# Attention of a two-layer block: values divided after 32 by 32 transposes on VectorE, rows of the mixture turned on TensorE, masks on ScalarE

## Chip, core and metric

The kernel runs on one core of a Trainium2 chip. The metric is the device time of one execution in microseconds (us). Engines: PE is TensorE, DVE is VectorE, ACT is ScalarE, POOL is GpSimd, SP is the engine whose queue issues most DMAs.

## What is computed

A block of two layers over x (8, 256, 256): an auto-correlation attention, a feed-forward layer with balanced experts, a multi-head attention over the context, and a mixture of 8 experts with the best two per token and a shared part. The change lies in the third, and in what hands its rows to the fourth:

```python
def _L1_xattn_ref(x, data, Wq, bq, Wkv, bkv, Wp, bp):
    # 8 batches, 256 queries, 256 keys, 16 heads of d = 16
    q = (x @ Wq + bq).reshape(bs, n_ctx, HEADS, d)
    kv = (data @ Wkv + bkv).reshape(bs, n_data, HEADS, 2 * d)
    k, v = (kv[..., :d], kv[..., d:])
    scores = jnp.einsum('bqhd,bkhd->bhqk', q, k) * scale
    attn = jax.nn.softmax(scores, axis=-1)
    out = jnp.einsum('bhqk,bkhd->bqhd', attn, v).reshape(bs, n_ctx, WIDTH)
    return out @ Wp + bp
...
    x = x + _L1_xattn_ref(_layernorm(x, axis=-1), ctx_1024, ...)
    x = x + _L1_ffn_ref(_layernorm(x, axis=-1), ...)
```

All numbers are float32. A general path for unusual inputs is in the program too and isn't executed here.

## The kernel before

Tokens lie on partitions: X holds 16 tiles of 128 tokens, batch b has tiles 2b and 2b + 1 (TPB = 2). The 16 heads are in NB = 2 columns c of 8; within a column head 2g + m has the 32 partitions of group g, and m picks one of two halves. Every instruction is issued in the order of the source on its engine's queue; the helpers below are called from one loop over b and c (L3018), written out by hand so that each engine finds work of another batch while it waits.

For batch b, in (b, 0) and (b, 1):
- scores (L2666): per block of 128 keys, four products of 32 rows each into two tiles of the pool ps_s, then two Exp on ScalarE into ex.
- values (L2685), one step later: 16 products of the keys' values with ex into pv. VA has 16 values, a column of ones and zeros per head, so that pv holds in each group of 32 partitions the 16 sums and, in the 17th row, the divisor.
- keep (L2698): DVE copies pv to ov. turn_back (L2702): TensorE turns ov of a batch in 8 transposes, DVE takes reciprocals and multiplies into on. turn_out (L2725): TensorE turns on back in 4 transposes, DVE copies to oT. project_out (L2737): 8 products with wp, DVE adds to X.
- turn_q (L2628) and queries (L2632) prepare the next batch: 4 transposes of the normalised rows, a copy hT, 4 products, and for each c two masked copies QM (m = 0 by ScalarE, m = 1 by DVE; for b + 1 = 1 both by DVE).
- batch_stats and norm_m write the normalised rows of batch b - 2, HP, for the mixture: statistics on DVE, powers and norms on POOL. take_apart_m (L2770) lets ScalarE part their 16-bit halves, two DMA transposes on SP's queue turn them, and join_m (L2785), one batch later, lets ScalarE join them to HT. The last two batches are turned by TensorE (turn_m, L2757, with the helper turn_pair, L2615) after the loop.
- route (L2843), a generator whose steps are called from b = 4 on (`gates`): per four tiles, TensorE's logits pl, a turn pt, DVE's choice of two experts (some 25 small instructions), counts pc on TensorE. send (L2939) then scatters one tile's rows to Td with an indirect DMA of POOL's queue, one after another.

PSUM has eight banks: ps_m has three tiles of one bank for turns, queries, projection and route; ps_s two tiles of two banks; ps_v one tile for pv.

After the loop the shared experts' first products (classic_up, L3237, tiles from ps_s) alternate with turn_back, turn_out and project_out of batch 7, turn_m and the last routes; then the experts run, whose rows are loaded from Td (load_rows, L3543).

Of the kernel before, what the change touches and what calls it, by code (L numbers as in the profile page):

```python
# [1086 lines left out]
def fast_path(  # L1087
# [1376 lines left out]
    for e in range(E - 1):  # L2464
        if e == 5:

            wpv = L1_xattn_Wp.rearrange("(c g m d) n -> m g d c n", c=NB, g=4, m=2)
            for m in range(2):
                for g in range(4):
                    r0 = 64 * m + DH * g  # L2470
                    nc.sync.dma_start(out=wp[r0 : r0 + DH], in_=wpv[m, g])
                    nc.sync.dma_start(
                        out=bvc[r0 : r0 + DH, :],
                        in_=bkv[:, 1, :].rearrange("(c g m) d -> m g d c", c=NB, g=4)[m, g],
                    )
# [67 lines left out]
    ps_m = banks.enter_context(tc.tile_pool(name="ps_m", bufs=3, space=PSUM))  # L2543
    ps_s = banks.enter_context(tc.tile_pool(name="ps_s", bufs=2, space=PSUM))
    ps_v = banks.enter_context(tc.tile_pool(name="ps_v", bufs=1, space=PSUM))
# [86 lines left out]
    def queries(b, c, eng=nc.scalar):  # L2632
        if c == 0:
            QM[b] = pq2.tile([P, NB, 2, S], F32, tag="QM", name="QM")
        pp = ps_m.tile([P, S], F32, tag="pm", name="pp")
        for kc in range(KC):
            nc.tensor.matmul(  # L2637
                pp,
                wq[:, kc, c * P : (c + 1) * P],
                hTs[b][:, kc, :],  # L2640
                start=(kc == 0),
                stop=(kc == KC - 1),
            )
        for m in range(2):
            if m == 0 and eng is nc.scalar:
                nc.scalar.activation(
                    QM[b][:, c, m, :],
                    pp,
                    AF.Identity,
                    bias=bqm[:, c, m : m + 1],  # L2650
                    scale=mask[:, m : m + 1],
                )
            else:
                nc.vector.tensor_scalar(  # L2654
                    QM[b][:, c, m, :],
                    pp,
                    mask[:, m : m + 1],
                    bqm[:, c, m : m + 1],
                    ALU.mult,
                    ALU.add,  # L2660
                )

    pex = at.enter_context(tc.tile_pool(name="pex", bufs=4))
    ex, pvs, ovs, ons, oTs = {}, {}, {}, {}, {}
# [20 lines left out]
    def values(b, c, m):  # L2685
        if m == 0:
            pvs[b, c] = ps_v.tile([P, 2, S], F32, tag="pv", name="pv")
# [10 lines left out]
    def keep(b, c):  # L2698
        ovs[b, c] = pxs.tile([P, 2, S], F32, tag="ov", name="ov", bufs=3)
        nc.vector.tensor_copy(ovs[b, c], pvs.pop((b, c)))  # L2700

    def turn_back(b):  # L2702

        on = pxs.tile([P, TPB, NB, 2, 4, DH], F32, tag="on", name="on")
        ons[b] = on
        for qt in range(TPB):
            pt = ps_m.tile([P, NB, 2, 4, HW], F32, tag="pm", name="pt")
            for c in range(NB):
                for m in range(2):
                    nc.tensor.transpose(  # L2710
                        pt[:, c, m].rearrange("p g w -> p (g w)"),
                        ovs[b, c][:, m, qt * P : (qt + 1) * P],
                        ident,
                    )
            pv = pt.rearrange("p c m g w -> p (c m g) w")
            rs = small.tile([P, H, 1], F32, tag="rs", name="rs")
            nc.vector.reciprocal(rs, pv[:, :, DH : DH + 1])
            nc.vector.tensor_tensor(
                on[:, qt].rearrange("p c m g d -> p (c m g) d"),
                pv[:, :, 0:DH],  # L2720
                rs.to_broadcast([P, H, DH]),
                ALU.mult,
            )

    def turn_out(b):  # L2725
        pt = ps_m.tile([P, NB, TPB, P], F32, tag="pm", name="pt")
        for c in range(NB):
            for qt in range(TPB):
                nc.tensor.transpose(
                    pt[:, c, qt, :],  # L2730
                    ons[b][:, qt, c].rearrange("p m g d -> p (m g d)"),
                    ident,
                )
        oTs[b] = pxs.tile([P, NB, TPB, P], F32, tag="oT", name="oT")
        nc.vector.tensor_copy(oTs[b], pt)

    def project_out(b):  # L2737
        pp = ps_m.tile([P, TPB, D], F32, tag="pm", name="pp")
        for qt in range(TPB):
            for c in range(NB):  # L2740
                nc.tensor.matmul(  # L2741
                    pp[:, qt, :],
                    oTs[b][:, c, qt, :],
# [13 lines left out]
    def turn_m(b):  # L2757
# [4 lines left out]
        )  # L2762

    def between_m(b, kc):
        return HT[:, kc, (b + 1) * S : (b + 3) * S].bitcast(U16)

    def take_apart_m(b):  # L2770
        parts = between_m(b, 0)
        nc.scalar.copy(
            parts.rearrange("p (r t d) -> p r t d", r=TPB, t=2),
            HP[:, TPB * b : TPB * (b + 1), 0:D]
            .bitcast(U16)
            .rearrange("p r (d t) -> p r t d", t=2),
        )
        turned = between_m(b, 1).rearrange("p (c q) -> p c q", q=S)
        for r in range(TPB):
            nc.sync.dma_start_transpose(  # L2780
                out=turned[:, :, r * P : (r + 1) * P],
                in_=parts[:, 2 * D * r : 2 * D * (r + 1)],
            )

    def join_m(b):  # L2785
        nc.scalar.copy(
            HT[:, :, b * S : (b + 1) * S]
            .bitcast(U16)
            .rearrange("p k (q t) -> p k q t", t=2),
            between_m(b, 1).rearrange("p (t k q) -> p k q t", t=2, k=KC),  # L2790
        )
# [212 lines left out]
    queries(0, 0)  # L3004
    queries(0, 1)
# [12 lines left out]
    for b in range(B):  # L3018
        for c in range(NB):
# [4 lines left out]
            if (b, c) == (3, 0):  # L3024
                router_weights()
            if prev:
                values(*prev, 0)
                values(*prev, 1)
                keep(*prev)
# [3 lines left out]
            elif b == 0:  # L3033
                turn_q(1)
            elif c == 0:
                if b + 1 < B:
                    turn_q(b + 1)
            else:
                turn_out(b - 1)
                if b >= 2:  # L3040
                    take_apart_m(b - 2)
            if c == 0 and b >= 3:
                join_m(b - 3)
# [11 lines left out]
            if (b, c) == (0, 1):  # L3055
                queries(1, 0, nc.vector)
                queries(1, 1, nc.vector)
                norm_q(2, nc.vector, nc.vector)
            if c == 0:
                if b >= 1:  # L3060
                    turn_back(b - 1)
                if 0 < b and b + 1 < B:
                    queries(b + 1, 0)
                    queries(b + 1, 1)
# [704 lines left out]
    keep(*prev)  # L3769
    join_m(B - 3)  # L3770
# [8 lines left out]
    turn_back(B - 1)  # L3779
    gate2 = route(2)  # L3780
    next(gate2)
    next(up0)
    turn_out(B - 1)
# [5 lines left out]
    send(2)  # L3789
    next(gate2)  # L3790
# [225 lines left out]
```

## Time and profile before

| | us |
|---|---|
| time, median of 3 runs (lowest to highest) | 806.14 (805.73 to 806.98) |
| the profiled execution | 805.7 |
| its span, first to last instruction | 804.0 |
| granted TensorE clock, mean | 0.998 |
| first scores, last values of the loop | 216.97, 330.28 |

The stage in stretches, cut where the values of a batch begin or end (busy time of each engine in the stretch):

| stretch | length | PE | DVE | ACT | POOL |
|---|---|---|---|---|---|
| 244.90:259.14, b = 2 | 14.24 | 14.24 | 9.06 | 10.41 | 8.07 |
| 259.14:273.34, b = 3 | 14.20 | 14.20 | 9.84 | 11.48 | 8.03 |
| 273.34:288.25, b = 4 | 14.91 | 14.91 | 11.05 | 11.63 | 8.12 |
| 288.25:303.65, b = 5 | 15.40 | 14.54 | 12.87 | 11.57 | 7.93 |
| 303.65:318.63, b = 6 | 14.98 | 14.98 | 8.93 | 11.70 | 8.11 |
| 318.63:332.20, b = 7 | 13.57 | 13.30 | 7.72 | 11.23 | 7.03 |
| 332.20:365.70, after the loop | 33.50 | 33.50 | 17.22 | 12.29 | 14.98 |

In the profile a line of the chain of waits gives start, length, engine, tile and source line, and the number of instructions; a float32 product shows as two of them, a transpose as one: x8 of scores are four products. A group's line gives the shapes out<-in, the count, the busy time and the mean ns of one, then the idle time before it and what ended that. A wait's line gives who waited for whom, the us in total, how often, and the longest. The matmul's end is modelled, so TensorE can look busy while it waits inside a group; a group that is longer than its sisters tells that.

### The profile page before, as it was taken

The numbers are of one execution on the slowest core, as the hardware profiler recorded it, in microseconds if no ns is written. First come the engines' busy times: TensorE is split into PE (matmuls) and PEld (weight loads), VectorE is DVE, ScalarE is ACT, GpSimd is POOL, SyncE is SP. The second block draws the span as 40 slices with busy tenths as digits, with TensorE's granted clock in tenths as the row PEclk, the third lists the DMA queues.
The fourth block names the chain that finished last, engine by engine and source line by source line (L and its number), as shares of the span: only waits on it lengthen the run. The fifth ranks groups of instructions, "written<-read, shape, count | busy, mean of one in ns | idle before, by whom it ended". The sixth has DMA issues, their size and how long they took to land.

```text
span 804.0 us, 13763 instructions
## 1 busy us (share of the span) xinstructions
PE 787.9 (98%) x5100; PEld 626.4 (78%) x5100; DVE 520.4 (65%) x1473; ACT 369.5 (46%) x676; POOL 214.8 (27%) x293
## 2 busy tenths in 40 slices
PE   7999999999999999999999999999999999999997
PEld 6547778788655555547898989798979898999986
DVE  5367877640466686456866686767676859686732
ACT  3344554234367777532425363444444545433330
POOL 6343122221136546533230001102122311202030
PEclk9999999999999999999999999999999999999999
DMA  8293666597161102161114585697759564311023
GB/s 263 76 313 101 215 192 188 182 264 227 53 184 28 27 18 57 41 210 61 48 48 114 172 248 167 178 298 212 184 133 297 108 196 110 111 14 20 8 32 130
DMA packets 111252, 111.16 MB, mean 138 GB/s; under 512 B 32936, under 2 KB 101768, under 8 KB 111144
## 3 DMA queue, kind: packets, MB, share of 16 engines
q1 hardware_dynamic: 102504, 96.87, 40.3%
q0 software_dynamic: 7920, 13.02, 7.8%
q8 instruction: 42, 0.69, 0.4%
q10 hardware_dynamic: 752, 0.30, 0.1%
q14 instruction: 34, 0.28, 0.1%
HBM read 80.61 MB, written 25.37 MB: 132 GB/s over the span
## 4 chain that ended last, share of the span: by engine, by line
PE 92%; DVE 3%; DMA 2%; issue 1%; ACT 1%; POOL 0%; ACTq 0%; SPq 0%; DVEq 0%
PE a L3286 19%; PE e L3286 9%; PE a L3345 9%; PE ph L2385 7%; PE py L2402 7%; PE B L3286 5%; PE e L3345 4%; PE p L2673 4%; PE pv L2690 3%; PE pgu L3248 3%; PE py L3491 3%; PE B L3345 2%; PE pp L1419 2%; PE pp L1398 2%; PE pp L2741 2%; PE pp L2637 1%
## 5 line engine op out<-in xcount | busy, mean ns | idle before, releaser
L3589 POOL DMA_INDIRECT Od<-Y,ids x32 | 50.8, 1587 | 279.0 <-DVE Y L3414 97.4
L3274 ACT COPY B<-a 128x512 f32<-128x512 f32 (+1 forms) x54 | 28.6, 531 | 168.4 <-PE a L3286 132.5
L2681 ACT ACTIVATE ex<-p,scale 128x1024 f32<-128x1024 f32 x64 | 67.8, 1110 | 25.3 <-PE p L2673 24.3
L3286 PE MATMUL a<-T,HP 128*128 128x256 f32 x288 | 73.9, 379 | 0.0
L3136 DVE TENSOR_TENSOR cc<-e,s 128x512 f32<-128x512 f32 x44 | 30.4, 691 | 56.1 <-PE e L3286 56.1
L3286 PE MATMUL a<-RT,wab 128*128 128x256 f32 x256 | 66.3, 381 | 0.0
L3136 DVE TENSOR_TENSOR act<-act 128x256 f32<-128x256 f32 (+1 forms) x120 | 61.4, 512 | 2.7
L2385 PE MATMUL ph<-RT,w 128*128 128x256 f32 x256 | 62.0, 390 | 0.0
L2402 PE MATMUL py<-w,A 128*128 128x256 f32 x256 | 61.6, 387 | 0.0
L3286 PEld LDWEIGHTS a<-T,HP 128*128 128x128 f32 x288 | 54.0, 190 | 7.0
L3286 PEld LDWEIGHTS a<-RT,wab 128*128 128x128 f32 x256 | 46.6, 190 | 7.3 <-issue 1.6
L2385 PEld LDWEIGHTS ph<-RT,w 128*128 128x128 f32 x256 | 45.1, 190 | 8.0 <-ACT RT L2370 0.5
L2402 PEld LDWEIGHTS py<-w,A 128*128 128x128 f32 x256 | 46.3, 190 | 6.1
L2394 ACT ACTIVATE A<-ph,b1c 128x256 f32<-128x256 f32 x64 | 30.3, 474 | 43.7 <-PE ph L2385 39.5
L2944 POOL DMA_INDIRECT Td<-HP,to x32 | 32.5, 1015 | 62.5 <-DMA Td<-HP,to 56.9
L2673 PE MATMUL p<-QM,KT 32*128 32x512 f32 x256 | 40.8, 639 | 1.0 <-DVE QM L2654 0.5
L3136 DVE TENSOR_TENSOR act<-act,cc 128x512 f32<-128x512 f32 x44 | 30.3, 689 | 13.4 <-ACT act L3320 13.1
L2412 POOL DMA_INDIRECT Yd<-Y,ids x16 | 15.8, 991 | 74.9 <-DVE Y L2411 21.5
L3301 ACT COPY s<-a 128x512 f32<-128x512 f32 x44 | 25.8, 587 | 20.0 <-PE a L3286 20.0
L3136 DVE TENSOR_TENSOR cc<-a,s 128x512 f32<-128x512 f32 x44 | 30.4, 691 | 3.8
L3286 PE MATMUL e<-RT,HP 128*128 128x256 f32 x128 | 32.9, 379 | 0.0
L3286 PE MATMUL e<-T,wab 128*128 128x256 f32 x128 | 32.8, 379 | 0.0
(522 smaller groups left out, 1730.2 us busy)
## 6 DMA issues: line engine op xcount, KB each, us to landing
w<-in_L_ffn_w_dram SPq DMA_DIRECT2D x16, 1024.0 KB, 10.3
wab<-in_L_ffn_w_e_dram SPq DMA_DIRECT2D x16, 1024.0 KB, 7.8
wc<-in_L_ffn_w_e_dram SPq DMA_DIRECT2D x8, 1024.0 KB
sab<-in_L_ffn_w_e_dram SPq DMA_DIRECT2D x32, 256.0 KB, 5.8
R<-Td SPq DMA_DIRECT2D x8, 530.0 KB
sc<-in_L_ffn_w_e_dram SPq DMA_DIRECT2D x16, 256.0 KB, 4.6
Td<-blank SPq DMA_DIRECT2D x2, 1590.0 KB, 10.0
X<-in_x_dram SPq DMA_DIRECT2D x4, 512.0 KB, 6.5
```

Of the source, the lines that this page charges most:

```text
L2385: nc.tensor.matmul(ph, w1[:, kc, f * P : (f + 1) * P], RT[:, kc, :], start=(kc == 0), stop=(kc == KC - 1),)
L2394: nc.scalar.activation(A[:, f, :], ph, AF.Gelu_apprx_tanh, bias=b1c[:, e, f : f + 1])
L2402: nc.tensor.matmul(py, A[:, f, r * P : (r + 1) * P], w2[:, f, :], start=(f == 0), stop=(f == NF - 1),)
L2673: nc.tensor.matmul(ps[g // 2][:, g % 2].rearrange("p m q -> p (m q)"), KT[rows, c, k0 : k0 + P], QM[b][rows, c].rearrange("p m q -> p (m q)"),
L2681: nc.scalar.activation(e4[:, 2 * j : 2 * j + 2], ps[j], AF.Exp, scale=scale)
L2944: nc.gpsimd.indirect_dma_start(out=Td, out_offset=bass.IndirectOffsetOnAxis(ap=to[g][:, k, j : j + 1], axis=0), in_=HP[:, GT * g + j, :], ...
L3136: eng.tensor_tensor(out, a, b, op)
L3274: nc.scalar.copy(self.b[:, 0 : self.n], self.a[:, 0 : self.n])
L3286: nc.tensor.matmul(ps[:, m * HT2 : (m + 1) * HT2], self.w.get(m, left, self.k), self.x.part[right], start=start and m == 0, stop=True, ski ...
L3301: nc.scalar.copy(self.s2, self.a)
L3345: nc.tensor.matmul(ps[:, qs], self.acts[k][:, left, qs], self.w.get(right, k), start=start and i == 0 and k == 0, stop=(k == NK - 1), skip ...
L3589: nc.gpsimd.indirect_dma_start(out=Od, out_offset=bass.IndirectOffsetOnAxis(ap=ids, axis=0), in_=Y, in_offset=None, compute_op=ALU.add,)
```

## The change

- values write pv into ps_m; keep, turn_back and turn_out are gone. divide(b, c), called right after the values, does it all on DVE: a transpose of pv in blocks of 32 by 32 to ov, reciprocals, the multiply to on, and a transpose back in such blocks to oT. The rows of wp and of the bias come in another order to fit.
- ps_m has two tiles, ps_s three, ps_v none.
- queries makes all four products into one tile first, and ScalarE makes all four masked copies (DVE for b + 1 = 1, as before).
- turn_q(b + 1) moves ahead of the values for b = 1 to 6; for b = 0 it stays behind them.
- take_apart_m and join_m with their DMA transposes are gone; turn_m(b - 2) on TensorE, with a copy by ScalarE, takes their place in (b, 1) from b = 2.
- After the loop project_out(7) comes one product group earlier.

```diff
-                    r0 = 64 * m + DH * g
+                    r0 = 2 * DH * g + DH * m
...
-    ps_m = banks.enter_context(tc.tile_pool(name="ps_m", bufs=3, space=PSUM))
-    ps_s = banks.enter_context(tc.tile_pool(name="ps_s", bufs=2, space=PSUM))
-    ps_v = banks.enter_context(tc.tile_pool(name="ps_v", bufs=1, space=PSUM))
+    ps_m = banks.enter_context(tc.tile_pool(name="ps_m", bufs=2, space=PSUM))
+    ps_s = banks.enter_context(tc.tile_pool(name="ps_s", bufs=3, space=PSUM))
...
+    def queries(b, eng=nc.scalar):
+        QM[b] = pq2.tile([P, NB, 2, S], F32, tag="QM", name="QM")
+        pp = ps_m.tile([P, NB, S], F32, tag="pm", name="pp")
+        for c in range(NB):
+            for kc in range(KC):
+                nc.tensor.matmul(
+                    pp[:, c],
+                    wq[:, kc, c * P : (c + 1) * P],
+                    hTs[b][:, kc, :],
+                    start=(kc == 0),
+                    stop=(kc == KC - 1),
+                )
+        for c in range(NB):
+            for m in range(2):
+                if eng is nc.scalar:
+                    nc.scalar.activation(
+                        QM[b][:, c, m, :],
+                        pp[:, c],
+                        AF.Identity,
+                        bias=bqm[:, c, m : m + 1],
+                        scale=mask[:, m : m + 1],
+                    )
...
-            pvs[b, c] = ps_v.tile([P, 2, S], F32, tag="pv", name="pv")
+            pvs[b, c] = ps_m.tile([P, 2, S], F32, tag="pm", name="pv")
...
+    def divide(b, c):
+        if c == 0:
+            oTs[b] = pxs.tile([P, NB, S], F32, tag="oT", name="oT")
+        ov = pxs.tile([P, 2, S // HW, HW], F32, tag="ov", name="ov")
+        rs = small.tile([P, 2, S // HW, 1], F32, tag="rs", name="rs")
+        on = pxs.tile([P, S // HW, 2, DH], F32, tag="on", name="on")
+        nc.vector.transpose(
+            ov.rearrange("p m n w -> p (m n w)"),
+            pvs.pop((b, c)).rearrange("p m q -> p (m q)"),
+        )
+        nc.vector.reciprocal(rs, ov[:, :, :, DH : DH + 1])
+        nc.vector.tensor_tensor(
+            on.rearrange("p n m d -> p m n d"),
+            ov[:, :, :, 0:DH],
+            rs.to_broadcast([P, 2, S // HW, DH]),
+            ALU.mult,
+        )
+        nc.vector.transpose(oTs[b][:, c], on.rearrange("p n m d -> p (n m d)"))
...
-    queries(0, 0)
-    queries(0, 1)
+    queries(0)
...
+            if c == 0 and 0 < b < B - 1:
+                turn_q(b + 1)
             if prev:
                 values(*prev, 0)
                 values(*prev, 1)
-                keep(*prev)
+                divide(*prev)
             send()
...
-            elif c == 0:
-                if b + 1 < B:
-                    turn_q(b + 1)
-            else:
-                turn_out(b - 1)
-                if b >= 2:
-                    take_apart_m(b - 2)
-            if c == 0 and b >= 3:
-                join_m(b - 3)
+            elif c == 1 and b >= 2:
+                turn_m(b - 2)
...
             if c == 0:
-                if b >= 1:
-                    turn_back(b - 1)
                 if 0 < b and b + 1 < B:
-                    queries(b + 1, 0)
-                    queries(b + 1, 1)
+                    queries(b + 1)
...
-    turn_back(B - 1)
     gate2 = route(2)
-    next(gate2)
-    next(up0)
-    turn_out(B - 1)
     next(gate2)
     next(up0)
     project_out(B - 1)
     batch_stats(B - 1, "m")
     norm_m(B - 1)
     send(2)
+    next(gate2)
+    next(up0)
     next(gate2)
     turn_m(B - 2)
```

More of the change, by code (lines that the diff above doesn't have):

```diff
@@ L2630, in turn_q @@
         turn_pair(h2s.pop(b), hTs[b], nc.vector.tensor_copy)
[L2632 to L2651, printed above, removed]
-                )
-            else:
[L2654 to L2661, printed above, removed]
+    def queries(b, eng=nc.scalar):
[9 more added lines that the diff above has]
+                    stop=(kc == KC - 1),
+                )
+        for c in range(NB):
[8 more added lines that the diff above has]
+                    )
+                else:
+                    nc.vector.tensor_scalar(
+                        QM[b][:, c, m, :],
+                        pp[:, c],
+                        mask[:, m : m + 1],
+                        bqm[:, c, m : m + 1],
+                        ALU.mult,
+                        ALU.add,
+                    )
@@ L2663, in fast_path @@
     pex = at.enter_context(tc.tile_pool(name="pex", bufs=4))
-    ex, pvs, ovs, ons, oTs = {}, {}, {}, {}, {}
+    ex, pvs, oTs = {}, {}, {}
     def scores(b, c, kt):
@@ L2696, in values @@
                 )
[L2698 to L2735, printed above, removed]
+    def divide(b, c):
[13 more added lines that the diff above has]
+            rs.to_broadcast([P, 2, S // HW, DH]),
+            ALU.mult,
+        )
+        nc.vector.transpose(oTs[b][:, c], on.rearrange("p n m d -> p (n m d)"))
@@ L2742, in project_out @@
                     pp[:, qt, :],
-                    oTs[b][:, c, qt, :],
+                    oTs[b][:, c, qt * P : (qt + 1) * P],
                     wp[:, c, :],
@@ L2761, in turn_m @@
             nc.scalar.copy,
[L2762 to L2790, printed above, removed]
         )
@@ L3034, in fast_path @@
                 turn_q(1)
-            elif c == 0:
-                if b + 1 < B:
-                    turn_q(b + 1)
-            else:
-                turn_out(b - 1)
-                if b >= 2:
-                    take_apart_m(b - 2)
-            if c == 0 and b >= 3:
-                join_m(b - 3)
+            elif c == 1 and b >= 2:
+                turn_m(b - 2)
             if gates:
@@ L3055, in fast_path @@
             if (b, c) == (0, 1):
-                queries(1, 0, nc.vector)
-                queries(1, 1, nc.vector)
+                queries(1, nc.vector)
                 norm_q(2, nc.vector, nc.vector)
             if c == 0:
-                if b >= 1:
-                    turn_back(b - 1)
                 if 0 < b and b + 1 < B:
-                    queries(b + 1, 0)
-                    queries(b + 1, 1)
+                    queries(b + 1)
                 if b + 2 < B and b:
@@ L3768, in fast_path @@
     values(*prev, 1)
-    keep(*prev)
-    join_m(B - 3)
+    divide(*prev)
     at.close()
```

## The prediction, made before the run

> **What bounds the kernel now.** I read the page's busy row and chain first, then the chain cut to the attention stage (217 to 332 us), then the groups there, the waits and the timelines.
>
> ```profile
> PE 787.9 (98%) x5100; PEld 626.4 (78%) x5100; DVE 520.4 (65%) x1473; ACT 369.5 (46%) x676; POOL 214.8 (27%) x293
> PE 92%; DVE 3%; DMA 2%; issue 1%; ACT 1%; POOL 0%; ACTq 0%; SPq 0%; DVEq 0%
> ```
>
> TensorE is the chain. One batch of attention in that chain (b = 3):
>
> ```profile
> 261.07 0.59 PE pt L2619 x4
> 261.66 1.07 PE p L2673 x8
> 262.73 1.02 PE pt L2710 x8
> 263.75 1.73 PE pp L2637 x8
> 265.48 1.07 PE p L2673 x8
> 266.55 1.86 PE pv L2690 x32
> 268.42 0.58 PE pt L2729 x4
> 269.00 1.07 PE p L2673 x8
> 270.07 1.93 PE pp L2741 x8
> 272.00 1.41 PE p L2673 x8
> ```
>
> With the values (1.86) that precede them these make the period of 14.2 us; TensorE never stops in it. The last scores take 1.41 where their sisters take 1.07. The list of waits says why (scores wait for a buffer of ps_s that Exp still reads):
>
> ```profile
> PEld p L2673 <- ACT ex L2681: 3.9, 11, 0.7
> ```
>
> In the batches with routing (b = 4 to 7) DVE shares the chain from 283.26 to 293.69: it is late there.
>
> **The change, part by part.** Sums are against the profiled execution (805.7, span 804.0); the median of the runs, 806.14, is 0.4 above.
>
> *Gone from TensorE.* turn_back: 7 x 1.02 + 0.87 = 8.0. turn_out: 7 x 0.59 + 0.44 = 4.6. Waits for ps_s, which gets a third buffer: 5 x 0.35 + 0.85 (b = 7) = 2.6. *Added:* turn_m for six batches, each as a turn of four (0.59): 3.5. Net 11.7 saved if nothing new waits. The twelve DMA transposes leave SP; nothing on the chain waited for them (one 0.5 wait by ACT), so I take 0.
>
> *VectorE.* Per batch it loses keep 2 x 0.69, turn_back 2 x (0.25 + 0.42), the oT copy 0.68 and two masks 2 x 0.54: 4.5. It gains two divides. Their prices, none of which stands as such in the trace, come from these groups:
>
> ```profile
> L2700 DVE COPY ov<-pv 128x512 f32<-128x512 f32 x16 | 11.0, 689 | 13.2 <-PE pv L2690 13.2
> L2718 DVE TENSOR_TENSOR on<-pt,rs 128x256 f32<-128x256 f32 x16 | 6.8, 425 | 0.6
> L2717 DVE RECIPROCAL rs<-pt 128x16 f32<-128x16 f32 x16 | 4.0, 252 | 4.6 <-PE pt L2710 4.6
> L2857 DVE COPY lT<-pl 128x128 f32<-128x128 f32 x3 | 0.8, 281 | 0.0
> ```
>
> A transpose of 128x512 is at least the copy of that shape, 0.69, one of 128x256 at least 0.42. [...] Nearer the copies, I take 0.72 + 0.25 + 0.42 + 0.45 and three hand-overs of 0.04 (L2717 to L2718 shows as much): 1.95 a divide, 3.9 a batch. VectorE stays below TensorE: in b = 2 it is busy 9.1 of 14.2, so 9.1 - 4.5 + 3.9 = 8.5 after.
>
> The multiply now has two SBUF inputs instead of one. [...]
>
> ```profile
> 285.60 0.19 DVE L2877 TENSOR_TENSOR pr__3453<-pr__3453,rsm 128x32 f32<-128x32 f32 x1
> 286.72 0.93 DVE L2891 TENSOR_TENSOR picks<-cand,first 128x32 f32<-128x32 f32 x1
> 284.89 1.36 POOL L2595 TENSOR_SCALAR h<-X,b_mv,b_r 128x256 f32<-128x256 f32 x1
> 286.33 1.27 POOL L2611 TENSOR_TENSOR X<-X,bpb 128x512 f32<-128x512 f32 x1
> ```
>
> L2877 ran its usual 0.19 under L2595; L2891 stood until L2611 ended. [...]
>
> *ScalarE.* Out: two 16-bit copies, 1.05 + 1.16. In: two masks more (0.56 each, 0.46 apart) and a copy of 0.59. About 11 of 12.8 us: not the bound, but all four masks of a batch now end about 2 us after the Exp before them.
>
> *New waits.* ps_m has two buffers, not three, and holds pv too. So each turn, values, queries and projection waits for the reader of the tile two before. A plain batch on TensorE is 4 x 1.07 + 2 x 1.86 + 2 x 0.59 + 1.73 + 1.93 = 12.8. I laid the queues out by hand in the built program's order with the durations above:
> - Start. queries(0) masks after all four products and on ScalarE alone: the first scores at 217.6 instead of 216.97. In (0,1) the hT copy stands behind divide (1.95 where keep took 0.6), so queries(1) ends at 229.2, its masks 1.9 later, then norm_q(2); TensorE waits for both. By scores (2,0,1) TensorE has been spared 2.0 and is only 0.85 ahead: 1.2 lost.
> - b = 3: router_weights' two products now use both buffers, and turn_q(4), moved ahead of the values, waits for the gwT copy, 2.9 after X's addition starts (257.78 to 260.56 now): 1.5.
> - b = 4 and 6: the route's product shifts the ring, and values wait for the masks: 0.6 + 0.7.
> - b = 5: VectorE still works off the route; values wait for the addition to X: 1.25. The route's pc waits for mk, now behind a whole divide: 1.55, where 0.95 is waited today. b = 7 likewise: 2.15 against 0.27.
> Sum: 1.2 + 1.5 + 1.3 + 1.25 + 0.6 + 1.9 = 7.7.
>
> In plain batches I find no wait: values follow the addition to X by about 0.9, turn_m the masks by 0.7, projection the transpose by 1. Cover gone, each us of lateness beyond these costs a us a batch.
>
> *Behind it.* The loop's end comes 2.7 earlier, the tail saves 1.3 (turn_back and turn_out of batch 7): 4.0. From 365.8 on TensorE runs without a gap, so this carries to the end if the rows arrive. They come by 32 indirect sends in POOL's queue, about 3 us each, up to 419.4; VectorE already waits 3.7 for the first rows (426.1). The queue starts with to[0], some 2 us earlier, and stops today 3.7 for batch 7's statistics, which come 7 us earlier: I find its end 5 to 6 earlier. What is late next is VectorE's backlog after each route.
>
> **The rivals.**
> (a) As laid out: 11.7 - 7.7 = 4.0, so 801.7 in the profile, 802.1 in the median. 0.45, covering 800 to 804.5.
> (b) The waits are half hidden (a turn or score fills them, the start recovers): about 8 gained, 798. For it: before's own waits in routes were only 1.2. Against: the orders in the queues are fixed. 0.13.
> (c) Transposes of 4-byte words at half speed: +0.8 a divide. On the path: start 0.8, b = 5 and b = 7 two divides each 3.2, pt of the routes 0.5. The gain is spent: 806.3. For it: no f32 transpose in the trace. Against: copies from PSUM take the same 0.69. 0.17.
> (d) Slower: VectorE becomes the bound in every batch. It has 4.6 of other work and 0.8 in each divide besides the transposes, so it passes 12.8 when the two transposes of a divide together take more than 3.3 us (I take 1.17), and 14.2, today's period, past 4.0. At fourfold (4.7) a batch costs 15.5: 1.3 more, 9 over seven batches, less what the tail saves: 814. [...] Against it: a third of VectorE's time is free in a plain batch. For it: every divide sits between two readers of a two-buffer ring. 0.25, most of it nearer 808 to 810.
> That the change does nothing it says is excluded: the built order has 96 transposes fewer and 24 more.
>
> **Numbers.** 806.14 - 4.0 = 802.1. This kernel's measurement tells about 0.2% (1.6 us) from no change. Faster: (a), (b) and a little of (c), 0.60; within: 0.15; slower: (d) and the rest of (c), 0.25. Range 798.5 to 809: from most of (b) to the near part of (d).
>
> **What would show it.** Right: the transposes at about 0.72 and 0.45; scores after a projection at 1.07 and no wait of scores for ex; a plain batch near 12.8; the first scores 0.6 later; waits of turn_q for gwT near 1.5, of pc for mk near 1.5 and 2; values of (7,1) ending near 329.5; the last send near 414. Wrong: transposes above 1.1; multiplies at 1 us or more under POOL's norms; values or queries that wait for DVE in b = 2 and 3; TensorE gaps after 420 on rows that come late.

## The result and the profile after

The changed kernel takes 807.49 us (median of 22 runs, 805.51 to 810.06) where the kernel before, run beside it, takes 806.49 (22 runs): a ratio of 1.0017, interval 1.001 to 1.0025. By the ratio it is slower by about 1.4 us (the medians lie 1.0 apart); I had forecast 4.0 less. Its profiled execution took 807.14, with a span of 805.4.

The busy row and the chain of the changed kernel, as on its page:

```profile
PE 780.1 (97%) x5028; PEld 618.2 (77%) x5028; DVE 517.0 (64%) x1467; ACT 365.4 (45%) x684; POOL 217.8 (27%) x293
PE 92%; DVE 4%; DMA 2%; issue 1%; POOL 0%; ACT 0%; SPq 0%; ACTq 0%; DVEq 0%
```

TensorE still is the chain. Its busy time is 7.8 us less and the span 1.4 longer: it waits more. The batch b = 3 from its chain (start, length, engine, tile, line, count), to be held against the one shown before:

```profile
264.46 1.07 PE p L2673 x8
265.53 1.92 PE pp L2636 x8
267.45 1.07 PE p L2673 x8
...
272.04 1.93 PE pp L2723 x8
273.97 1.07 PE p L2673 x8
```

turn_back is gone, scores take 1.07 each time, and the period is 13.03 (264.39 to 277.42 in the timeline) instead of 14.2. But queries take 1.92 where they took 1.73. VectorE's divide, from the groups of the page:

```profile
L2706 DVE STREAM_TRANSPOSE ov<-pv 128x512 f32<-128x512 f32 x16 | 11.5, 717 | 24.2 <-PE pv L2690 24.0
L2717 DVE STREAM_TRANSPOSE oT<-on 128x256 f32<-128x256 f32 x16 | 7.1, 445 | 0.6
L2711 DVE TENSOR_TENSOR on<-ov,rs 128x256 f32<-128x256 f32 x16 | 7.0, 439 | 0.6
```

717 and 445 ns are the prices I took; rivals (c) and (d) need about twice and four times that. So VectorE's part went as forecast, and the plain batch came within 0.2 of it. What went wrong is told by TensorE's list of waits (for whom, us in total, times, longest) and by the timeline of the first batch (start, length, instructions, and in brackets the wait ahead):

```profile
PE pc L2855 <- DVE mk L2851: 3.3, 2, 1.8
PE pt L2618 <- DVE gwT L2792: 1.9, 1, 1.9
...
PE pp L2636 <- DVE hT L2621: 1.0, 1, 1.0
PE pv L2690 <- DVE X L2731: 1.0, 1, 1.0
```

```profile
208.43 1.03 PE L2944 MATMUL pbp<-wp,bvc 128*128 128x256 f32 x4
...
211.86 1.99 PE L1419 MATMUL pp<-wkv_in,CT 128*128 128x256 f32 x8 [0.68 <-ACT VA L1428]
214.53 0.66 PE L2618 MATMUL pt<-ident,h 128*128 128x128 f32 x4 [0.68 <-ACT VA L1428]
216.29 1.96 PE L2636 MATMUL pp<-hT,wq 128*128 128x256 f32 x8 [1.10 <-DVE hT L2625]
219.50 1.14 PE L2673 MATMUL p<-QM,KT 32*128 32x512 f32 x8 [1.25 <-ACT QM L2646]
```

The same in the kernel before (between these lines it waits once, 0.77 for the copy hT):

```profile
208.80 1.03 PE L2991 MATMUL pbp<-wp,bvc 128*128 128x256 f32 x4
...
216.97 1.14 PE L2673 MATMUL p<-QM,KT 32*128 32x512 f32 x8 [0.51 <-DVE QM L2654]
```

In the changed kernel pbp sits in one of the two tiles of ps_m, which are handed out in turn (a ring of two), from 208.43 until VectorE adds it to bpb at 215.95. Meanwhile the two products of the values and the first turn share the other tile, and each waits for the reader of the one before. First scores come 11.07 after pbp; before it was 8.17.

The second thing is the granted clock. The timeline of b = 7, and the stretches around it (length; busy of PE, PEld, DVE, ACT, POOL; then PEclk, the DMA's share and GB/s):

```profile
323.80 0.18 PE L2855 MATMUL pc<-mk,ones_b 128*128 128x32 bf16 x1 [1.76 <-DVE mk L2851]
...
325.00 3.29 PE L2690 MATMUL pv<-ex,VA 128*32 128x256 f32 x32
328.23 0.93 PE L2618 MATMUL pt<-ident,HP 128*128 128x128 f32 x4
```

```profile
322.00:324.00 2.00, 0.24 (x10) 0.23 (x6) 1.81 (x8) 1.86 (x2) 1.61 (x5) 1.00 0.00 0
...
326.00:328.00 2.00, 2.00 (x24) 0.79 (x16) 0.00 (x0) 1.29 (x2) 1.10 (x1) 0.50 0.14 53
```

After a wait of 1.76 (0.27 in the kernel before) TensorE runs at half clock from 325.42 to 328.83 (from stretches of 0.2 us), so values take 3.29 instead of 1.93 and the turn 0.93 instead of 0.66: 1.6 us that no wait's length shows. The prediction has no such term.

### The profile page after: what moved, and what is told of

It is laid out like the page before. It is cut to its first block, busy times and chain, and to the rows that moved or that the text cites. A ratio compares the mean times of both kernels' runs of the same rounds, so it can differ in the third digit from the quotient of the medians.

```text
span 805.4 us, 13595 instructions
## 1 busy us (share of the span) xinstructions
PE 780.1 (97%) x5028; PEld 618.2 (77%) x5028; DVE 517.0 (64%) x1467; ACT 365.4 (45%) x684; POOL 217.8 (27%) x293
## 4 chain that ended last, share of the span: by engine, by line
PE 92%; DVE 4%; DMA 2%; issue 1%; POOL 0%; ACT 0%; SPq 0%; ACTq 0%; DVEq 0%
PE a L3229 19%; PE e L3229 9%; PE a L3288 9%; PE ph L2385 7%; PE py L2402 7%; PE B L3229 5%; PE e L3288 4%; PE pv L2690 4%; PE p L2673 4%; PE pgu L3191 3%; PE py L3434 3%; PE B L3288 2%; PE pp L2636 2%; PE pp L1419 2%; PE pp L1398 2%; PE pp L2723 2%
## 5 line engine op out<-in xcount | busy, mean ns | idle before, releaser
L2673 PE MATMUL p<-QM,KT 32*128 32x512 f32 x256 | 37.0, 639 | 2.4 <-ACT QM L2646 1.2
L3079 DVE TENSOR_TENSOR act<-act,cc 128x512 f32<-128x512 f32 x44 | 30.3, 688 | 13.3 <-ACT act L3263 13.1
L2690 PE MATMUL pv<-ex,VA 128*32 128x256 f32 x512 | 32.3, 395 | 1.0 <-DVE X L2731 1.0
L3229 PE MATMUL B<-RT,wab 128*128 128x256 f32 x128 | 32.8, 379 | 0.0
```

Source lines behind the costliest of these rows:

```text
L2673: nc.tensor.matmul(ps[g // 2][:, g % 2].rearrange("p m q -> p (m q)"), KT[rows, c, k0 : k0 + P], QM[b][rows, c].rearrange("p m q -> p (m q)"),
L2690: nc.tensor.matmul(pvs[b, c][32 * g : 32 * g + 32, m, :], VA[:, b * TPB + kt, 8 * c + 2 * g + m, :], ex[b, c, kt][:, g, m, :], start=(kt = ...
L3079: eng.tensor_tensor(out, a, b, op)
L3229: nc.tensor.matmul(ps[:, m * HT2 : (m + 1) * HT2], self.w.get(m, left, self.k), self.x.part[right], start=start and m == 0, stop=True, ski ...
```

## The experiments

Every kernel was timed beside the kernel before on the same chip, so the ratios can be compared and the medians less so. Below, **loop** is the time in the profile from pbp's first product to the first product after the loop, and a **fall** is a stretch of 3.41 us at half clock (PEclk 0.50), worth up to half of it, 1.7 us:

| kernel | ratio (interval) | loop | falls in it |
|---|---|---|---|
| before | 1 | 123.34 | 0 |
| changed | 1.0017 (1.001 to 1.0025) | 125.52 | 1 |
| bias added early | 1.0002 (0.9994 to 1.001) | 122.92 | 0 |
| pbp in ps_s | 1.0001 (0.9992 to 1.0009) | 123.21 | 1 |
| mk first | 1.0001 (0.9985 to 1.0016) | 125.05 | 2 |
| router moved | 0.9977 (0.9966 to 0.9988) | 121.74 | 0 |
| four tiles, two | 1.0037 (1.0022 to 1.0051) | 127.87 | 2 |
| DMA transposes back | 1.0031 (1.0019 to 1.0043) | 125.27 | 2 |
| delay in before | 1.0023 (1.0014 to 1.0031) | 124.84 | 0 |
| division alone | 1.0015 (1.0004 to 1.0025) | 126.12 | 1 |
| and turn_q ahead | 0.9969 (0.9958 to 0.998) | 123.92 | 2 |
| and mk first | 0.9925 (0.9912 to 0.9939) | 118.91 | 0 |
| all mends, first try | 0.9975 (0.9963 to 0.9987) | 121.29 | 1 |
| mended | 0.9923 (0.9909 to 0.9936) | 117.18 | 0 |
| mended, DMA transposes | 0.9899 (0.9884 to 0.9914) | 116.59 | 1 |
| mended, short wait | 0.993 (0.9917 to 0.9944) | 117.59 | 0 |
| mended, long wait | 0.9977 (0.9965 to 0.999) | 121.85 | 2 |

### The start: the bias added early, and pbp in another pool

```diff
+    nc.vector.tensor_tensor(bpb, bpb, pbp, ALU.add)
     for i in range(0, 4, 2):
         list(vals(i, 2, ps_m))
     norm_q(0, nc.vector, nc.vector)
...
-    nc.vector.tensor_tensor(bpb, bpb, pbp, ALU.add)
```

> The changed kernel with one line moved: VectorE adds the bias product pbp to bpb before the values' products of the first batch, not after the first turn, so that pbp leaves its bank at once. Theory (a ring of two with one bank blocked costs the start): TensorE no longer waits 0.68 + 0.68 for ACT VA at 211.9 and 214.5; first scores near 217.7 instead of 219.50; the wait of queries(1) for hT grows from 0.98 by what TensorE comes earlier, since hT stands behind divide, so that 0.8 to 1.8 remain at the loop's end: about 806.2 against 807.5. Rival (the start is set by ScalarE's masks and VectorE's norms, not by the bank): first scores stay within 0.3 of 219.5 and the time stays.

First scores came 10.34 after pbp, 0.7 earlier than in the changed kernel, not 1.8: the addition, first in VectorE's queue after the statistics, stood behind their wait for a power from POOL, and TensorE waited 1.15 for bpb instead of twice 0.68 for VA. The theory was half right. The tile need not be in this ring at all:

```diff
-    pbp = ps_m.tile([P, D], F32, tag="pm", name="pbp")
+    pbp = ps_s.tile([P, D], F32, tag="p", name="pbp")
```

> The changed kernel with pbp in a tile of ps_s instead of ps_m (ps_s is idle until the first scores); the addition to bpb stays where it was. Theory (pbp holds one of two ps_m tiles from 208.4 to 216): both waits for VA (0.68 each) go, hT is waited for 0.77 instead of 1.10, first scores 1.7 earlier against pbp than in the changed kernel (11.1 after pbp's start there, 9.4 here); as TensorE waited 1.79 within 3.4 us there, falls of the clock at 217 go too. (0,1) gives part of it back, the rest reaches the end: ratio 0.9995 to 1.0005. Rival (VectorE sets the start): first scores within 0.4 of 11.1 after pbp, ratio 1.0017.

First scores 9.01 after pbp, both waits for VA gone, hT waited for 0.77: the theory's picture, with 2.1 won where it had 1.7. By scores (2,0,1) these 2.1 are still there. The ratio fell by 0.0016, 1.3 us.

### The route: mk ahead of divide, and the router's weights elsewhere

```diff
             scores(b, c, 0)
+            if gates and c == 0:
+                next(gates, None)
...
-            if gates:
+            if gates and c == 1:
                 next(gates, None)
```

> The changed kernel with the step of route that ends in mk called right after the first scores of (5,0) and (7,0), ahead of divide on VectorE's queue. Theory (a wait of TensorE costs its length, and once it is long enough the granted clock falls to half for some 3.3 us and costs 1.6 more): both waits of pc for mk, 1.52 and 1.76, go; no half clock at 325 to 328; values of (7,0) 1.93 instead of 3.29; time lower by 2.5 to 4.5, near 803.5, and granted clocks of 0.996 or more in most executions. Rival 1 (the clock falls on its own): the half clock is still there in the loop, time lower by at most 3. Rival 2 (waits only change place, VectorE being late): divide, now 0.6 later, makes values or pt wait as long, time within 1 of 807.5.

Both waits for mk are gone and no wait took their place, so Rival 2's reason is out. But the ratio fell by 0.0016 only, 1.3 us and not the theory's 2.5 to 4.5, and half clock is still in the loop: that is what Rival 1 had said, and this run alone doesn't rule it out. The profiled execution had two other falls, after the waits at the start and for gwT, and the 22 executions stand apart: seven at 802.8 to 803.1, six at 804.3 to 804.8, eight at 806.8 to 808.1 and one at 814.3, with mean clocks of 0.997 to 1.0 in the first two groups, 0.991 to 0.993 in the third and 0.989 in the last. If waits bring the falls, they have to be removed together; whether they do is tested at the end.

```diff
-            if (b, c) == (3, 0):
-                router_weights()
...
             else:
+                if b == 2:
+                    router_weights()
                 if b >= 1:
                     project_out(b - 1)
...
+        pc = ps_m.tile([P, KC, E], F32, tag="pm", name="pc")
         for kc in range(KC):
-            pc = ps_m.tile([P, E], F32, tag="pm", name="pc")
-            nc.tensor.transpose(pc, gw[:, kc * P : (kc + 1) * P], ident[:E, :E])
-            nc.vector.tensor_copy(gwT[:, kc, 0:E], pc)
+            nc.tensor.transpose(pc[:, kc], gw[:, kc * P : (kc + 1) * P], ident[:E, :E])
+        nc.vector.tensor_copy(gwT[:, :, 0:E], pc)
```

> The changed kernel with router_weights called in (2,1) ahead of the projection, its two small turns in one tile of ps_m with one copy. Theory (turn_q(4) waits only because two tiles of a ring of two are taken at once and their copies stand late in VectorE's queue; a wait over some 1.7 can also cost a 3.41 us stretch at half clock): the wait of 1.91 for gwT goes, no wait over 0.3 takes its place, 1.9 less in executions without a fall of the clock, up to 3.6 less in those where this wait caused one: ratio to the kernel before near 0.999 instead of 1.0017. Rival (the wait only moves to the projection or to values of the next step, since VectorE is behind there): ratio within 0.001 of 1.0017.

The wait of 1.91 went without a successor, the loop has no fall, and the ratio fell by 0.0040, 3.2 us: 1.9 for the wait; the rest I take for falls, which this run doesn't show apart. Moving this single call turns the loss into a gain.

### The banks

```diff
-    ps_m = banks.enter_context(tc.tile_pool(name="ps_m", bufs=2, space=PSUM))
-    ps_s = banks.enter_context(tc.tile_pool(name="ps_s", bufs=3, space=PSUM))
+    ps_m = banks.enter_context(tc.tile_pool(name="ps_m", bufs=4, space=PSUM))
+    ps_s = banks.enter_context(tc.tile_pool(name="ps_s", bufs=2, space=PSUM))
```

> The changed kernel with four tiles in ps_m and two in ps_s instead of two and three (all eight banks in use either way). Theory (the new waits are the price of the ring of two): the waits for VA at the start (2 x 0.68), for gwT (1.91), for X in b = 5 (0.95) and for ov (2 x 0.25) go; first scores near 218; scores wait for Exp again, 0.3 to 0.4 twice a batch, about 5 in all; the two waits for mk stay: ratio 1.000 to 1.002, with fewer falls of the clock. Rival (the order on VectorE's queue sets the waits, not the number of tiles): waits for gwT, X and ov stay within 0.3 of what they are and the scores' waits come on top: ratio 1.005 or more.

The waits for VA, gwT, X and ov all vanished, as the theory said: they are the price of two tiles. But the ratio is 1.0037 and not 1.000 to 1.002: the profile has two falls where I expected fewer, and the scores' waits cost more than I gave them. From its timeline:

```profile
265.98 1.54 PE L2673 MATMUL p<-QM,KT 32*128 32x512 f32 x8
...
269.89 1.45 PE L2673 MATMUL p<-QM,KT 32*128 32x512 f32 x8
```

Scores of 1.45 and 1.54 where the changed kernel has 1.14 (overlap included): a plain batch takes 13.8 and not 13.0. The third tile of scores is worth 0.8 a batch and the choice of banks was right for the plain batch; what cost time was what else went into the ring of two.

### The mixture's turn: DMA transposes back

```diff
             elif c == 1 and b >= 2:
-                turn_m(b - 2)
+                take_apart_m(b - 2)
+            if c == 0 and b >= 3:
+                join_m(b - 3)
```

> The changed kernel with the mixture's rows of batches 0 to 5 turned as before, by take_apart_m, DMA transposes and join_m, instead of turn_m on TensorE. TensorE loses six turns of 0.59, 3.5 in all; ScalarE trades a copy of 0.59 for two of 1.05 and 1.16. Theory (ScalarE would be the bound: 8 Exp of 1.11, 4 masks of 0.56 and 2.2 of 16-bit copies are 13.3 a batch, where TensorE has 12.4): a plain batch takes 13.3 or more instead of 13.0, scores wait for masks or Exp, ratio 1.003 to 1.008. Rival (the six turns were paid in full): a plain batch 12.5, ratio 0.997 to 0.998.

Neither held whole. A plain batch took 12.76 (b = 3, 267.14 to 279.90), so ScalarE is not the bound and my 13.3 was wrong. Yet the ratio, 1.0031, is the theory's, with mean clocks of 0.990 to 0.993 in all six executions and two falls in the profiled loop. I put the ratio down to falls; this run doesn't show it. The exchange was repeated in the mended kernel (below).

### The division alone, on the kernel before

keep, turn_back and turn_out are replaced by divide, and wp's rows put in its order; nothing else:

```diff
-                keep(*prev)
+                divide(*prev)
...
-            else:
-                turn_out(b - 1)
-                if b >= 2:
-                    take_apart_m(b - 2)
+            elif b >= 2:
+                take_apart_m(b - 2)
...
-                if b >= 1:
-                    turn_back(b - 1)
```

> The kernel before with the division alone changed: divide with 32 by 32 transposes on VectorE in place of keep, turn_back and turn_out; banks (3, 2 x 2, 1), masks on both engines, DMA transposes and the order of calls as before. Theory (the division's part is the gain, the rest of the change gave it back): turn_back and turn_out leave TensorE, less 0.2 per batch that queries take over as the first full-array products after scores; scores then follow each other sooner and wait more for Exp with two buffers, so a plain batch takes 13.2 to 13.6 (14.2 before, 13.0 changed); the start stays as before (first scores near 217); pc waits for mk about 1.5 in b = 5 and 7 and the clock may fall once. 801 to 804. Rival (VectorE's longer chain is what eats the gain): waits for DVE in b = 2 and 3 as well, no faster than 806.

The theory is refuted in its number and the rival is right that waits for VectorE come in every batch, though for another reason than its load. VectorE in b = 2, from its timeline, and what TensorE makes of it:

```profile
248.64 0.45 DVE L2715 STREAM_TRANSPOSE oT<-on 128x256 f32<-128x256 f32 x1
249.01 0.65 DVE L2622 COPY hT<-pt 128x512 f32<-128x512 f32 x1
251.48 0.54 DVE L2654 TENSOR_SCALAR QM<-pp,mask,bqm 128x256 f32<-128x256 f32 x1 [1.82 <-ACT QM L2646]
```

```profile
PE pp L2637 <- DVE hT L2622: 6.3, 6, 1.2
```

The copy hT stands behind the longer divide; VectorE then idles for 1.82. It is order, not load. So the next run calls turn_q ahead of the values, as the full change does:

```diff
+            if c == 0 and 0 < b < B - 1:
+                turn_q(b + 1)
             if prev:
                 values(*prev, 0)
```

> The kernel before with the division alone changed, as in the run of the division alone, and turn_q(2) to turn_q(7) called ahead of the values as in the full change; banks, masks and DMA transposes as before. Theory (in the division alone the copy hT stood behind the longer divide and queries waited 0.98 to 1.18 six times): these six waits go; scores that follow queries wait for Exp about 0.35 each instead; a plain batch 13.3 (14.0 in the division alone); pc waits for mk stay near 1.5 to 1.9: ratio near 0.997. Rival (ScalarE is the bound with two tiles of scores and the two 16-bit copies): the six waits turn into waits for Exp of the same size and the ratio stays at 1.0015 within 0.0015.

Five of the six waits went (the first, of 1.2 for b = 1, is not touched), a plain batch takes 13.2, and the ratio is the 0.997 of the theory. Two falls stay, behind waits for mk of 2.07 and 1.52. The last step puts mk ahead, with the edit of the run above:

> The kernel before with the division on VectorE, turn_q ahead of the values, and the route's step that ends in mk called ahead of the values' divide; banks, masks and DMA transposes as before. Theory (waits for mk of 2.07 and 1.52, with two falls of the clock of 1.7 each in the profile of the run without this step, were what the division's part still lost): both waits and both falls go: 3.6 to 6 less than that run's 0.9969, ratio 0.990 to 0.993, the fastest of all. Rival (scores wait for Exp with two tiles, so that TensorE runs into ScalarE instead): waits of scores for Exp grow by as much, ratio 0.995 or more.

0.9925, with no fall in the loop. Of the 5.0 by which the loop shrinks, up to 3.4 are the two falls; so of the 3.6 of waits as little as 1.6 was gained, since scores now wait for Exp in the same place (1.05 in b = 7). So 0.9925 comes from the division and two moves in the order. Banks, masks and turn_m had no part in it.

### All mends

The edits for mk, the router's weights and pbp together, and:

```diff
-                if eng is nc.scalar:
+                if eng is nc.scalar and (m == 0 or b > 1):
...
-            if c == 0 and 0 < b < B - 1:
+            if (b, c) == (0, 1) or c == 0 and 0 < b < B - 1:
                 turn_q(b + 1)
...
-                queries(1, nc.vector)
+                queries(1)
```

> The changed kernel with all waits that were found mended: pbp in a tile of ps_s; masks of b = 0 and 1 on both engines; turn_q(1) ahead of the values; router_weights in (2,1) with one tile; the route's step that ends in mk ahead of divide. Theory (what the change gives TensorE, about 9.4 without the clock, is real, and orders and rings gave it back): first scores near 217.3, no wait of TensorE over 1.1 between 217 and 333, clock at 1.00 there in every execution, loop's end 7 to 9 earlier than before: ratio 0.990 to 0.993. Rival 1 (VectorE or ScalarE is the bound once TensorE is freed): a plain batch stays at 13.0 but the waits of the start and the routes come back for other reasons, ratio 0.996 to 0.999. Rival 2 (the experts wait for rows, the sends end no earlier): gaps on TensorE after 420 and ratio above 0.996.

The routes held: no wait over 0.95 from b = 2 on. The start did not. With masks given to VectorE and turn_q(1) ahead of the values, TensorE waited 2.25 for VectorE's copy VA at 225.72, and the clock fell from 226.41 on. So turn_q(1) went between values and divide, and the masks of b = 0 stayed on ScalarE:

```diff
                 values(*prev, 1)
+                if (b, c) == (0, 1):
+                    turn_q(1)
                 divide(*prev)
```

> The changed kernel with router_weights in (2,1) as one tile, the step that ends in mk ahead of divide, pbp in a tile of ps_s, turn_q(1) between values and divide, and the masks of b = 1 on both engines; unlike the run of all mends the masks of b = 0 stay on ScalarE and turn_q(1) comes after the values. Theory (in that run VectorE's queue in the first step was made the bound; waits of over half a stretch of 3.41 us halve the clock): no wait of TensorE over 1.3 between 215 and 333 and no fall of the clock there; the wait for VA of 2.25 goes; ratio 0.993 to 0.995. Rival (what is gained at the start is lost again in the first two batches, VectorE having a fixed amount of work there): scores of (2,0) not earlier against pbp than in the run of all mends, ratio 0.997 or more.

799.0 (798.77 to 799.34) where before has 805.25: 0.9923, a little better than the theory's 0.993 to 0.995. The loop is 6.2 shorter than before and 8.3 shorter than the changed kernel's. The longest waits that TensorE still has from the first queries on:

```profile
PE p L2673 <- DVE QM L2654: 1.3, 1, 1.3
PE p L2673 <- ACT QM L2646: 1.2, 1, 1.2
...
PE pv L2690 <- DVE X L2731: 1.0, 1, 1.0
```

On this kernel, the DMA transposes again (the diff is that of the exchange above):

> The mended kernel with the mixture's rows of batches 0 to 5 turned by take_apart_m, DMA transposes and join_m instead of turn_m. In the run of that exchange on the changed kernel a plain batch took 12.73 instead of 13.03, but falls of the clock hid what it gave. Theory (TensorE is the bound, the exchange saves 0.3 a batch, half of each turn, the rest going into waits of scores for Exp): loop 115.2 to 116 from pbp to the first product after it, 117.18 in the mended kernel; ratio 0.990 to 0.9915. Rival (ScalarE with 13.3 of work a batch is the bound where no wait leaves it room): loop 117 or longer, ratio 0.992 to 0.996.

797.06 (796.2 to 798.21), 0.9899, the fastest of all by a little: its interval and that of the mended kernel overlap. The loop is 116.59 with a fall in it, some 114.9 without, a little below the theory's 115.2. The batches b = 2 and 3 take 0.4 less each, so turn_m on TensorE costs about 2 us here, not nothing and not its full 3.5.

### Does a wait cost the clock?

First on the kernel before, where six scratch operations delay mk in b = 7:

```diff
+            if (b, c) == (7, 0):
+                late = pxs.tile([P, D // 2], F32, tag="late", name="late", bufs=1)
+                for i in range(6):
+                    nc.vector.tensor_scalar(
+                        late, X[:, i, 0 : D // 2], mask[:, 0:1], bqm[:, 0, 0:1], ALU.mult, ALU.add
+                    )
```

> The kernel before, with six small scratch copies (128x128, some 0.25 to 0.3 each) put on VectorE in (7,0) ahead of the route's step that ends in mk; the scratch is read by nobody. TensorE's wait for mk there, 0.27 today, becomes about 1.8. Theory (a long wait takes the clock with it): in part of the executions the granted clock is half for some 3.4 us after it, mean clock 0.996 or less there, and the time is 1.5 longer, or 3.1 with the fall: median near 808.5, and executions further apart than those of the kernel before. Rival (the wait costs its length alone): near 807.9 with the clock at 0.998 throughout.

The operations took 0.35 each, TensorE waited 2.48, and no fall followed: the rival's picture in the profile, though the wait was longer than those that had brought a fall so far. The time rose by 1.9. The executions form two groups, 806.4 to 806.5 and 807.8 to 808.3; but their mean clocks overlap, and the kernel before has such groups too (804.5 to 805.9 and 806.3 to 807.1), so they say nothing of falls.

The traces suggest why no fall came. Up to the end of the loop, every fall in every profile lasts 3.41 us or two such stretches, and those of one profile lie on one grid: in the changed kernel 11.40 to 14.81 and 325.42 to 328.83, which starts 92 stretches later. I laid that grid over each profile that has a fall and summed TensorE's waits in each stretch from 212 to 333:

| waited in the stretch | stretches | half clock in the next |
|---|---|---|
| 1.76 to 2.28 | 12 | 11 |
| 1.52 to 1.68 | 9 | 3 |
| under 1.5 | all others | 1 (right behind a fall) |

Of the two stretches with 1.76, one has a fall behind it (the changed kernel) and one has none (DMA transposes back). The start of the execution fits: from 5 to 16 us all six stretches with 1.86 to 2.30 are followed by a fall, and none with 1.70 or less except right behind one. One place does not fit. Around 40 us five profiles have a fall behind a stretch with only 0.67 to 0.96 of waiting, and others none behind as much as 1.07. TensorE makes narrow products there (32 and 8 columns), so the sum of waits can't be all that counts; what else does is open, and the table's limit holds for this loop.

The wait of 2.48 lay across a border of the grid, 1.19 on one side and 1.29 on the other. To test the rule rather than fit it (the table holds these runs too, one of the 12 and none of the 9), two waits were put into the mended kernel, whose executions lie within 0.6 of each other:

```diff
-            if gates and c == 0:
+            if gates and c == 0 and b < 7:
                 next(gates, None)
...
-            if gates and c == 1:
+            if gates and (c == 1 or b == 7):
                 next(gates, None)
```

> The mended kernel with the step that ends in mk put back behind divide for b = 7 alone, so that TensorE waits some 1.5 there once. The mended kernel's executions lie within 0.6 of each other. Theory (the clock halves for 3.41 us after a stretch of the fixed 3.41 grid with more than some 1.6 of waiting): the wait adds its 1.5, executions at 800.3 to 801, at most a third of them 1.7 later. Rival (any wait of over 1 costs the clock): most executions at 802 or more. Rival 2 (the falls are independent of waits): as in the theory for this run, but then also no more of them in the run with the long wait.

The long wait has the same edit and four of the scratch operations shown above.

> As the run with the short wait, with four scratch operations (0.35 each, read by nobody) on VectorE ahead of the step that ends in mk, so that TensorE waits some 2.9 there. Theory (grid of 3.41, fall beyond some 1.6 of waiting in one stretch: a wait of 2.9 placed at random leaves more than that in one stretch in four of five cases): 1.4 more than with the short wait where the clock stays, 3.1 more in most executions: a median near 803.6 to 804 against some 800.6. Rival 2 (the falls are independent of waits): a median 1.4 above the short wait's, executions as close together as the mended kernel's.

The short wait (1.53) gave 799.14 to 799.68, 0.0007 above the mended kernel: no group apart and no fall in the loop, and only 0.4 of the wait reaches the loop's end, since without it the scores that follow wait for Exp (they take 2.31 in the mended kernel, 1.14 here). So the theory's 800.3 to 801 was too high, for a cover that it left out, and the rival's 802 or more is refuted. The long one (2.92), from its timeline and its stretches:

```profile
320.66 0.19 PE L2855 MATMUL pc<-mk,ones_b 128*128 128x32 bf16 x1 [2.92 <-DVE mk L2851]
...
322.82 3.64 PE L2690 MATMUL pv<-ex,VA 128*32 128x256 f32 x32
```

```profile
319.00:321.00 2.00, 0.34 (x6) 0.30 (x9) 1.82 (x8) 0.95 (x1) 2.00 (x2) 0.75 0.00 0
...
323.00:325.00 2.00, 2.00 (x24) 0.85 (x24) 0.00 (x0) 2.00 (x2) 0.44 (x1) 0.50 0.19 68
325.00:327.00 2.00, 2.00 (x20) 0.96 (x12) 0.46 (x1) 0.11 (x1) 0.54 (x1) 0.54 0.19 68
```

The median is 803.42, and the 13 executions spread from 800.86 to 806.07: two at 800.9 (1.2 to 1.3 above the short wait's median, clock 0.998), four at 802.4 to 802.6, three at 803.4 to 803.7, four at 805.3 to 806.1 (clock 0.992). A wait 1.4 longer made the median 3.8 longer and the executions ten times as far apart. The times and the clocks move together (0.998 at 800.9, 0.993 to 0.996 at 802.4 to 802.6, 0.992 above): that is the theory, and rival 2, which expected 1.4 and no spread, is out. The profile shows two stretches in a row at half clock, more than the theory had.

What the runs show, then: with 1.76 to 2.28 of waiting within one stretch of this loop, 11 of 12 were followed by half clock.

## Why the prediction was wrong

- **Right: the mechanism of the gain.** Divide's prices, the shape of the batch (13.03 against 12.8), VectorE's busy time (8.38 in the batch of 13.03 against 8.5), no wait of values or queries for VectorE in b = 2 and 3 apart from the router's, the tail's 1.3 (1.36), and no gap on TensorE behind it. The last send at 416.3 was 3.1 earlier than before, where I had 5 to 6; nothing waited for it. (Rival (c)'s "+0.8 a divide" is not the 1.17 that twice 0.72 + 0.45 adds; with 717 and 445 ns measured, nothing rests on it.) No row of the kernel before shows the 0.72 and 0.45 of my sum, where its copy and its multiply of these shapes take 0.69 and 0.42, and no run shows the half speed of (c): the changed kernel's transposes took 717 and 445 ns.
- **Failed: the start** ("first scores at 217.6", "1.2 lost"). My ring held the right two tiles but not pbp, which is taken ahead of the loop. (Times of the start are counted from pbp.) First scores came at 219.50, 11.07 after pbp where 217.6 meant 8.8; by scores (2,0,1) TensorE was 2.4 behind the kernel before and not 0.85 ahead: 3.2. With pbp in ps_s it is 0.3 behind there, so pbp's tile is 2.1 of the 3.2; the mended kernel is 0.3 ahead, which is another 0.6 for the order of turn_q(1) and the masks. The last 0.6 is open.
- **Failed: the sum of waits has no clock in it.** The fall after the wait of b = 7 added 1.6 in the profile. In the 22 executions the mean clock runs from 0.998 down to 0.992, the slower ones having the lower clock on the whole; the two added waits show that such a spread comes with a long wait. The rest of the sum was fair in size: gwT 1.91 (1.5), X 0.95 (1.25), mk 1.52 and 1.76 (1.55 and 2.15).
- **Mis-sized: "turn_back: 7 x 1.02".** The row was right, but 0.15 to 0.19 of it seems to be the price of the first full-array products after the row-tiled scores (each product on 32 rows of the array): turn_back behind other work took 0.87. Without it queries pay (1.92 for 1.73), five times behind scores (2,0,1): 1.0. Only the before and after rows show this; no run isolates it.
- **Failed the other way: b = 4 and 6**, where I had 0.6 + 0.7 of values waiting for masks. Only pt waited, 0.25 each. Why the ring's order was easier than I took it was not tried.

Together, for the loop: 3.2 + 1.6 + 1.0 + 0.4 (gwT) - 0.8 (b = 4 and 6) - 0.7 (b = 5 and 7) = 4.7, of the 4.9 between my 2.7 saved and the 2.2 lost in the profile. The tail gives 1.4 of it back and this execution reached pbp 0.4 earlier, so that TensorE stays 0.45 late to its end, and the last write to memory took 0.9 longer in this execution; what made that is open.

The result, 807.49, lies between the 806.3 of rival (c) and the 808 to 814 of rival (d), but neither is its cause: both rest on a price of VectorE's transposes that was not paid, and the 808 to 810 of (d) on multiplies held for 1 us under POOL's norms besides, which the changed kernel doesn't show (0.42 to 0.43, one 0.65). Inside my range of 798.5 to 809 it is there by luck, not by (a). In the kernel before, the order in the queues suited a short keep and three tiles. The change put a long divide and two tiles into that order; with the mends above the same change gives 0.9923. The division with two calls moved gives 0.9925, the same within the intervals, so no net gain of the other banks, the masks on ScalarE and turn_m is shown.

## What to carry to other kernels

When an operation on a queue gets longer, look for what stands behind it and is waited for soonest, and move that ahead: two calls moved made the division alone go from 1.0015 to 0.9925. When a ring of tiles gets shorter, list everything that takes a tile from it, the calls ahead of the loop too. And look at TensorE's waits by stretches of 3.41 us and not one by one: in this loop half clock, up to 1.7 us beside the wait, followed 11 of the 12 stretches with 1.76 to 2.28 of waiting, 3 of the 9 with 1.52 to 1.68, and with less than 1.5 only one, right behind a fall.

## What I had not expected of the hardware

- Half clock (PEclk 0.50) for 3.41 us, or two such stretches, on a grid (11.40 and 325.42 in the changed kernel, 92 stretches apart), after 1.76 to 2.28 us of waiting in one stretch of it in 11 of 12 cases and after 1.52 to 1.68 in 3 of 9, in this loop. With mk ahead the executions of one kernel lay 5.4 us apart (802.8 to 808.1, one at 814.3 aside), with the long wait 5.2, in the mended kernel 0.6.
- The switch from row-tiled scores (32 rows) to full-array products seems to cost TensorE 0.15 to 0.2, whichever of these groups comes next: turn_back 1.02 behind scores and 0.87 behind other work, turn_out 0.59 and 0.44, project_out 1.93 and 1.73. The shared experts' eight products show as much behind tiles of 32 columns: 3.63 behind pl, 3.44 behind a turn. From the kernel before, behind the shared experts' products:

```profile
335.84 0.87 PE pt L2710 x8
...
337.29 3.63 PE pgu L3248 x8
340.92 0.44 PE pt L2729 x4
...
341.47 3.44 PE pgu L3248 x8
344.90 1.73 PE pp L2741 x8
```

- A multiply of 128x32 on VectorE took 1.06 instead of 0.19 to 0.21 beside POOL's addition to X, as L2891 (0.93) did in the trace before. Beside POOL's norms five multiplies of divide took their usual 0.42 to 0.43 and one 0.65 (at 308.47, the norm lasting to 309.52): none was held to the norm's end. From the two timelines of the changed kernel:

```profile
287.04 1.06 DVE L2830 TENSOR_TENSOR pr__3405<-pr__3405,rsm 128x32 f32<-128x32 f32 x1
286.78 1.27 POOL L2610 TENSOR_TENSOR X<-X,bpb 128x512 f32<-128x512 f32 x1 [2.00 <-DVE h L2594]
```
